# Attention and expert layer on one core: every transposition moves from the DMA queue to TensorE

## The chip, the cores and the metric

The kernel runs on one core of one Trainium2 chip. The time is the device time of one execution in microseconds (us); less is better. Before the change it is 672.57 us, the median of 3 runs that lie between 672.4 and 672.64 us. The engines are named as the profile names them: PE (TensorE, matrix products), PEld (its path for loading the stationary operand), DVE (VectorE), ACT (ScalarE), POOL (GpSimd), SP (SyncE, which here only issues DMAs).

## What is computed

One post-norm layer over x of shape (2, 512, 512): two batches of 512 positions with 512 features. Attention has 32 query heads and 8 key/value heads of 128 features each, with a causal mask. Behind it stands a dense layer with eight low-rank experts whose weights come from a sparsemax.

```python
q = (x @ Wq)  # 32 heads of 128
k = (x @ Wk)  # 8 heads, each serves 4 query heads
v = (x @ Wv)
scores = where(causal, einsum('bhqd,bhkd->bhqk', q, k) * scale, -inf)
out = softmax(scores) @ v
x = layernorm(x + out @ Wo)
base = x @ W_base.T + b_base
weights = sparsemax(x @ W_router.T + b_router)
expert = einsum('bser,bse,ero->bso', einsum('bsd,edr->bser', x, lora_A), weights, lora_B)
x = layernorm(x + base + expert)
```

## The kernel before

**Two halves of everything.** Every operand of a product is kept as two float16 numbers, a high and a low part, and a product a·b is made of three matmuls: high·high, high·low and low·high (`mm3`, L228). That is why matmul counts are multiples of three. Only key/value group 0 is projected in another way, directly from float32 data (`park`, the `xr`/`wr` tiles), while the scales of the split are still being found.

**Groups and units.** There are 16 groups (g, b): 8 key/value heads g by 2 batches b. A group has four units i = 0 to 3. Unit i is a block of 128 rows of each of the four query heads, that is, positions 128·i to 128·i+127, and it attends to the keys up to its own end. So unit 0 is the smallest and unit 3 the largest.

**The work of a group.** `proj` (L321) makes K (`j` = 4), V (`j` = 5) and four Q heads (`j` = 0 to 3) out of the transposed x: 12 matmuls of 512 columns each into a PSUM tile of the tag "pj", which has two buffers. `cut_psum` (L233) empties that tile: ACT writes the high half, then DVE the low half. V comes out of `mul_v` with features on the partitions, so it must be transposed: `turn_v` (L303) makes three more variants of it with four ACT copies (L312 to L315: `twice`, `once`, `four`, packings for the diagonal blocks) and one DMA transposition of all 20 blocks (L318).

**The work of a unit.** `unit_a` (L333): scores S (12 matmuls of 32 to 512 columns, into tag "S", four buffers), a minimum by DVE (L396), the exponential by ACT (L401), and then `cut_p`, which writes P's high and low halves into the tile `phl` (ACT L360, L368; DVE L363), as 8·i+6 float16 blocks of 128 by 128. Two DMA transpositions a unit (L389) turn those blocks into `pt`. `unit_b` (L416): P·V, 6 to 24 matmuls of 128 or 256 columns, with `vt` as the stationary and `pt` as the moving operand, into the tag "PV" (one buffer), emptied by `cut_psum` into `o`. `unit_c` (L457): 12 matmuls of 512 columns with the output weights into the tag "wo" (one buffer), and DVE adds the result to the residual row `acc` (L470).

**The order.** The main loop (L932) runs over steps s. A step does `unit_a` of unit s; then, for the next group, some of its six projections (`(4, 0)`, `(1,)`, `(5,)`, `(2, 3)` in the steps with i = 0, 1, 2, 3); then `unit_b` of unit s−1; then `unit_c` of unit s−2. In between, `advance` prepares weights for later groups on POOL (`split16`: three instructions a tile, L119, L121, L122). Within this loop a planner sets the final order of each engine's queue; each engine executes its queue in order. `sync_load` puts loads on SP's queue behind the third last transposition (`hist`).

**The end.** The last group and the second halves of the tiles of rows run in an order written out by hand (`TAIL`, L895): a letter is a piece of work, the digit a tile of 128 rows (`a`, `p`, `q`: `unit_a`; `b`, `o`: `unit_b`; `c`, `d`: `unit_c`; `X`, `l`, `r`, `s`, `h`, `m`, `e`, `f`, `F`: the expert layer). The expert layer needs the normalized x transposed: `turn(t, True)` lets TensorE transpose four float32 blocks of a tile (L596, ACT L598, DVE L607), for tiles 3 to 7. For tiles 0 to 2 (`ffn`, L672) x is split first (ACT L602, POOL L609) and transposed by DMA (L610).

PSUM has eight buffers of 2 KB a partition, all taken: two "pj", four "S", one "PV", one "wo".

Of the kernel before, what the change touches and what calls it, by code (L numbers as in the profile page):

```python
# [17 lines left out]
P = 128  # L18
# [22 lines left out]
def kernel(  # L41
# [50 lines left out]
    def f(ap):  # L92
        return ap.bitcast(F32)

    hist = []
# [158 lines left out]
    def cut(b, g, j):  # L254
        return CUT if g else CK[b][:, j : j + 1]
# [38 lines left out]

    def mul_v(g, b, tag="pj"):
        pv = pj(f"pvp{g}_{b}", tag)
        project(pv, g, b, 5)
        return pv

    def end_v(g, b, pv):  # L300
        cut_psum(v2[:, 0, :], v2[:, 1, :], pv, cut(b, g, 5))

    def turn_v(g, b):  # L303


        r = 2 * R
        high, low, twice, once, four = (v2[:, k, :].rearrange("p (t k) -> p t k", k=P) for k in range(5))

        def double(t, k):
            return high[:, :, :k].unsqueeze(2).broadcast_to([P, NT, t, k])  # L310

        nc.scalar.copy(twice.rearrange("p t (a k) -> p t a k", a=2), double(2, r))  # L312
        nc.scalar.copy(once[:, :, :r], low[:, :, :r])
        nc.scalar.copy(four.rearrange("p t (a k) -> p t a k", a=4)[:, :, ::3], double(2, R))
        nc.scalar.copy(four[:, :, R:r], low[:, :, :R])  # L315
        vt = sb.tile([P, 5 * NT, P], F16, tag="VT", name=f"vt{g}_{b}", bufs=2)
        with tc.issue_after(hist[-1]) if g == 0 and hist else nullcontext():
            sync_transpose(vt, v2.rearrange("p a s -> p (a s)"))  # L318
        VT[(g, b)] = vt

    def proj(g, b, j):  # L321
        if j == 4:
# [5 lines left out]
        else:  # L328
            end_q(g, b, j, mul_q(g, b, j))

    PT = {}

    def unit_a(g, b, i, whole=True):  # L333

# [7 lines left out]
        pt = sb.tile([P, nb, P], F16, tag="PT", name=f"pt{g}_{b}_{i}", bufs=2)  # L342
        es = []
        st = sb.tile([P, 4, 4], F32, tag="ast", name=f"ast{g}_{b}_{i}", bufs=3)
        full = i * P
# [1 line left out]
        def cut_p(h):  # L347
# [5 lines left out]
            for j in (h, h + 1):  # L353
# [30 lines left out]
                if i:  # L384
                    low(lows[:, :full], 0, full)
                low(p[:, full + (3 - j) * R : full + P][:, : n - full], full, n - full)

            on = slice(0, 2 * m) if h == 0 else slice(2 * m, nb)
            sync_transpose(pt[:, on], phl[:, on.start * P : on.stop * P])  # L389

        for j in range(4):
            n = full + (j + 1) * R
            qh, ql = (q2[:, a, HPG * i + j].rearrange("p h q -> p (h q)") for a in range(2))
# [10 lines left out]
            es.append(sc)  # L404
            if whole and j % 2:
                cut_p(j - 1)
        PT[(g, b, i)] = pt
        yield
        if not whole:
            for h in (0, 2):  # L410
                cut_p(h)
                yield

    OT = {}

    def unit_b(g, b, i):  # L416
        vt = VT[(g, b)]
        pt = PT.pop((g, b, i))
        pv = ps.tile([P, HPG, 4, R], F32, tag="PV", name=f"pv{g}_{b}_{i}")
        dst = pv.rearrange("p h j q -> p j h q")  # L420
        m = 2 * i + 1

        def blocks(start, step):
            return pt[:, start : start + step + 1 : step].rearrange("p j (h q) -> p j h q", q=R)

        def three(kt, start, step):
            vh, vl = vt[:, kt, :], vt[:, NT + kt, :]
# [9 lines left out]
        twice, once, four = (vt[:, k * NT + i, :] for k in (2, 3, 4))  # L437
# [152 lines left out]
    def turn(t, urgent=False):  # L590
        a = acc[t]
        X[t] = x2 = sb.tile([P, 2 * KC, P], F16, tag="raw", name=f"x2{t}", bufs=6)
        if urgent:
            px = ps.tile([P, KC, P], F32, tag="S", name=f"px{t}", bufs=4)
            for c in range(KC):
                nc.tensor.transpose(px[:, c, :], a[:, c * P : (c + 1) * P], ident)  # L596
            H[t] = px
            nc.scalar.copy(x2[:, :KC, :], px)  # L598
        else:
            xn = sb.tile([P, 2, HID], F16, tag="raw", name=f"xn{t}", bufs=6)  # L600
            H[t] = xn
            nc.scalar.copy(xn[:, 0], a)  # L602

    def low(t, engine):
        x2, src = X[t], H[t]
        if src.dtype == F32:
            nc.vector.tensor_tensor(x2[:, KC:, :], src, x2[:, :KC, :], ALU.subtract)  # L607
        else:
            engine.tensor_tensor(src[:, 1], acc[t], src[:, 0], ALU.subtract)  # L609
            sync_transpose(x2, src.rearrange("p a d -> p (a d)"))  # L610

    PA, PB, H = {}, {}, {}

# [58 lines left out]
    def ffn(t):  # L672
# [2 lines left out]
        yield  # L675
        with behind(mybir.EngineType.DVE):
            normalize(a, a, st)
        turn(t)
        low(t, nc.gpsimd)
        for _ in range(5):  # L680
            yield
        with behind(mybir.EngineType.PE):
            lora_in(t, False)
# [209 lines left out]


    TAIL = """  # L895
    n3 a7 C6 N3 B7 p7 q7 O7 X3 l3 D6 a6 r3 C7 s3 b7 p6 q6 D7 h3 o7 m3 a5 p5 c7 b6 q5 e3 d7 o6 n7
    a4 c6 N7 p4 q4 b5 f3 X7 l7 m7 o5 r7 d6 n6 s7 c5 N6 d5 h7 X6 n5 l6 b4 e7 o4 f7 r6 c4 N5 F7 s6
    F3 X5 l5 d4 n4 m6 h6 r5 m5 s5 N4 e6 f6 h5 X4 l4 F6 e5 r4 s4 f5 m4 h4 F5 e4 f4 F4
    """

    def tail():
# [2 lines left out]
        A = {first + i: unit_a(g, b, i, False) for i in range(NT)}  # L904
        B = {first + i: unit_b(g, b, i) for i in range(NT)}
        C = {first + i: unit_c(g, b, i, i == NT - 1) for i in range(NT)}
        B6 = {first + NT - 1: unit_b(*groups[-2], NT - 1)}
        C6 = {first + i: unit_c(*groups[-2], i, False) for i in (NT - 2, NT - 1)}
        pieces = dict.fromkeys("apq", A) | dict.fromkeys("bo", B) | dict.fromkeys("cd", C)
        pieces |= dict.fromkeys("BO", B6) | dict.fromkeys("CD", C6)  # L910
        work = {
            "l": lambda t: low(t, nc.vector), "L": lambda t: low(t, nc.gpsimd),
            "s": route, "e": lora_part, "x": turn, "X": lambda t: turn(t, True),
            "r": lambda t: lora_in(t, t >= NT), "m": lambda t: base_part(t, True), "h": lambda t: lora_mid(t, t >= NT),
        }
        stats = {}
# [15 lines left out]
    for s in range(len(units) - NT):  # L932
        if s < len(units):
            g, b, i = units[s]
            k = s // NT
            nx = groups[k + 1] if k + 1 < len(groups) else None
            done(unit_a(g, b, i))
            step_live()
            if nx:
                for j in ((4, 0), (1,), (5,), (2, 3))[i]:  # L940
                    proj(*nx, j)
                    advance()
            step_live()
        if s >= LB:
            done(unit_b(*units[s - LB]))
            step_live()
            advance()
# [66 lines left out]
```

## Time and profile before

| | |
|---|---|
| median of 3 runs | 672.57 us (672.4 to 672.64) |
| the profiled execution, its own time | 674.08 us |
| its span, first to last instruction | 672.3 us |
| mean granted TensorE clock | 0.996 |
| transposing DMAs | 128 of P, 16 of V, 3 of x, all on SP's queue |
| median from issue to landing | P 3.6 us, V 5.3 us, x 2.9 us |
| POOL, instructions before the change | 405 |

The profile is of one execution, whose time is 1.5 us above the median; 1.8 us of it lie outside the span. A group of instructions is given as line, engine, operation, what it writes and reads, count, busy time and the mean duration of one. A matmul's duration reaches from its start until its last result has drained; matmuls that follow each other overlap, so the distance between two starts is what one of them costs the engine, and it is found from a run of n matmuls as (length of the run − duration of one) / (n − 1).

### The profile page before, as it was taken

What the parts mean: (1) busy time and instruction counts of PE and PEld (TensorE: products, weight loads), DVE (VectorE), ACT (ScalarE), POOL (GpSimd) and SP (SyncE); (2) the same over time, 40 slices, a digit from 0 to 9 for tenths busy, and PEclk for the clock granted to TensorE, in tenths of its full rate; (3) what the DMA queues carried; (4) which work ended last, traced back from release to release, by engine and by line L of the source; (5) the groups of instructions that cost most, each with busy time, mean ns of one, the idle gap of its engine ahead of it and who ended that gap; (6) DMA issues with size and microseconds to landing.
All of it is one profiled execution on the core that took longest, in us unless ns stands there. A gap on an engine that the chain in (4) does not pass through costs nothing. (4 is left out here: it accounts for less than half of the span.)

```text
span 672.3 us, 12440 instructions
## 1 busy us (share of the span) xinstructions
PE 652.2 (97%) x3946; PEld 374.7 (56%) x3946; DVE 520.8 (77%) x1698; ACT 388.5 (58%) x1196; POOL 259.2 (39%) x405
## 2 busy tenths in 40 slices
PE   8899999999999999999999999999899999999995
PEld 5666555555555555555555655555465555555552
DVE  5788687968696686978788787868767687878796
ACT  6886574847374774747466475726656484545510
POOL 5658550634227199543318058053505011100011
PEclk9899999999999999999999999999999999999999
DMA  8659483656739374655739363653828164563311
GB/s 310 173 158 208 100 182 78 148 84 128 147 63 231 89 148 101 115 130 98 177 40 254 74 145 72 129 146 58 176 39 142 24 126 75 88 129 75 71 40 52
DMA packets 213538, 81.06 MB, mean 121 GB/s; under 512 B 198112, under 2 KB 198368, under 8 KB 213472
## 3 DMA queue, kind: packets, MB, share of 16 engines
q1 hardware_dynamic: 213472, 80.26, 56.2%
q8 instruction: 31, 0.51, 0.3%
q14 instruction: 35, 0.29, 0.2%
HBM read 29.12 MB, written 2.10 MB: 46 GB/s over the span
## 5 line engine op out<-in xcount | busy, mean ns | idle before, releaser
L401 ACT ACTIVATE s<-s,ast 128x320 f32<-128x320 f32 (+15 forms) x256 | 117.6, 460 | 149.8 <-DVE ast L396 145.1
L231 PE MATMUL pw<-w,o 128*128 128x512 f16 x768 | 177.0, 379 | 0.3 <-DVE acc L470 0.3
L231 PEld LDWEIGHTS <-w 128*128 128x128 f16 x1008 | 98.0, 98 | 110.7
L231 PE MATMUL pq<-xT,w 128*128 128x512 f16 x672 | 152.4, 379 | 0.0
L363 DVE SCALAR_TENSOR_TENSOR phl<-s,ast,phl 128x128 f16<-128x128 f32 (+7 forms) x352 | 125.1, 417 | 33.9 <-ACT phl L360 31.3
L360 ACT ACTIVATE phl<-s,ast 128x96 f16<-128x96 f32 (+11 forms) x304 | 117.3, 478 | 9.1 <-DVE ast L350 6.0
L231 PEld LDWEIGHTS <-o 128*128 128x128 f16 x768 | 74.8, 98 | 77.8 <-issue 0.8
L396 DVE CUSTOM_DVE_ANT_0 s<-s,mask,lm 128x320 f32<-128x320 f32 (+15 forms) x256 | 113.3, 502 | 1.9 <-PE s L231 1.3
L231 PE MATMUL s<-k,q 128*128 128x480 f16 (+15 forms) x768 | 103.1, 279 | 5.7 <-DVE phl L363 1.9
L231 PE MATMUL pv<-pt,vt 128*128 128x256 f16 (+1 forms) x960 | 105.6, 262 | 2.9 <-DMA pt<-phl 1.5
L231 PEld LDWEIGHTS <-vt 128*128 128x128 f16 x960 | 86.1, 99 | 22.5 <-issue 4.3
L231 PEld LDWEIGHTS <-q 128*128 128x128 f16 x768 | 62.7, 98 | 45.3 <-issue 4.1
L263 POOL TENSOR_SCALAR lm<-sc,xs 128x1 f32<-128x1 f32 x15 | 4.0, 268 | 206.7 <-DVE sc L139 103.0
L122 POOL TENSOR_TENSOR w<-raw,w 128x512 f16<-128x512 f32 x70 | 79.8, 1164 | 0.2
L119 POOL TENSOR_SCALAR raw<-raw,sc 128x512 f32<-128x512 f32 x70 | 48.0, 698 | 53.6 <-issue 39.0
L470 DVE SCALAR_TENSOR_TENSOR acc<-pw,lm,acc 128x512 f32<-128x512 f32 x64 | 47.7, 745 | 19.6 <-PE pw L231 19.3
L236 DVE SCALAR_TENSOR_TENSOR o<-pv,o 128x512 f16<-128x512 f32 x64 | 43.6, 682 | 24.1 <-ACT o L235 24.0
L235 ACT ACTIVATE o<-pv 128x512 f16<-128x512 f32 x64 | 40.0, 625 | 24.3 <-PE pv L231 24.1
L401 ACT ACTIVATION_READ_ACCUMULATOR s<-s,ast 128x1 f32 x256 | 51.3, 200 | 0.0
L125 DVE TENSOR_REDUCE mx<-raw 128x1 f32<-128x512 f32 x68 | 44.1, 675 | 8.0 <-DMA raw<-in_wo_dram 7.8
L236 DVE SCALAR_TENSOR_TENSOR q<-pq,q 128x512 f16<-128x512 f32 x56 | 37.4, 682 | 9.5 <-ACT q L235 9.5
L348 DVE RECIPROCAL ast<-ast 128x2 f32<-128x2 f32 x128 | 20.9, 163 | 29.8 <-ACT s L401 28.5
(172 smaller groups left out, 675.3 us busy)
## 6 DMA issues: line engine op xcount, KB each, us to landing
raw<-in_wo_dram SPq DMA_DIRECT2D x32, 256.0 KB, 3.4
raw<-in_wq_dram SPq DMA_DIRECT2D x29, 256.0 KB, 4.6
xraw<-in_xt_dram SPq DMA_DIRECT2D x8, 256.0 KB, 5.2
raw<-in_wk_dram SPq DMA_DIRECT2D x8, 256.0 KB, 3.8
raw_x<-in_xt_dram SPq DMA_DIRECT2D x8, 256.0 KB, 4.7
acc<-in_x_dram SPq DMA_DIRECT2D x8, 256.0 KB, 5.1
pt<-phl SPq DMA_TRANSPOSE x128, 3.6
out_dram<-y SPq DMA_DIRECT2D x8, 256.0 KB, 2.0
```

Of the source, the lines that this page charges most:

```text
L119: nc.gpsimd.tensor_scalar(view, view, by, 1.0, ALU.mult, ALU.mult)
L122: return first.ins, nc.gpsimd.tensor_tensor(lo, view, hi, ALU.subtract).ins
L125: nc.vector.tensor_reduce(dst, view, AX.X, ALU.max, apply_absolute_value=True)
L231: nc.tensor.matmul(dst, a, b, start=first and j == 0, stop=last and j == n - 1)
L235: nc.scalar.activation(hi, psrc, AF.Copy, scale=by)
L236: return nc.vector.scalar_tensor_tensor(lo, psrc, by, hi, ALU.mult, ALU.subtract).ins
L348: nc.vector.reciprocal(st[:, 2, h : h + 2], st[:, 1, h : h + 2])
L360: nc.scalar.activation(dst, src, AF.Copy, scale=by)
L363: nc.vector.scalar_tensor_tensor(dst, src[:, at : at + k], by, p[:, at : at + k], ALU.mult, ALU.subtract)
L396: nc.vector.tensor_tensor_reduce(out=sc[:, :n], in0=sc[:, :n], in1=mask[:, S - n :], scale=lm[:, 0:1], scalar=BIG, op0=ALU.add, op1=ALU.mi ...
L401: nc.scalar.activation(sc[:, :n], sc[:, :n], AF.Exp, bias=st[:, 0, j : j + 1], scale=-1.0, accum_out=st[:, 1, j : j + 1])
L470: nc.vector.scalar_tensor_tensor(a, pw, LM[(g, b)][:, 7:8], a, ALU.mult, ALU.add)
```

## The change

No DMA transposes any more; `hist` and `sync_transpose` go, and loads are no longer held behind transpositions.

*P.* A new generator `unit_t` has TensorE transpose the blocks of `phl`, eight at a time, against a float16 identity (`ident16`, made once by POOL) into a PSUM tile `px`, and ACT copies that tile to `pt` (`turn_blocks`). In the main loop its first pieces stand before the projections of the step, one piece before each projection; what is left comes right before `unit_b`, which now stands behind `unit_c`. `px` takes the tag "pj" in the main loop.

*V.* For g > 0 `mul_v` exchanges the operands: x is stationary, the weights move, so keys come out on the partitions and no transposition is needed; it takes 48 matmuls of 128 columns in place of 12 of 512. For g = 0 TensorE transposes the eight blocks. The variants `twice`, `once`, `four` are made by six POOL copies in place of four ACT copies, in two standing tiles `vts`, of which each group uses the other.

*x.* `turn` always goes through TensorE, and `low` always through DVE, also for tiles 0 to 2.

*The end.* `T` and `t` in `TAIL` are the pieces of `unit_t`.

```diff
-    v2 = const.tile([P, 5, S], F16, tag="v2", name="v2")
-    nc.gpsimd.memset(v2[:, 3:, :], 0.0)
+    ident16 = const.tile([P, P], F16, tag="ident16", name="ident16")
+    nc.gpsimd.tensor_scalar(ident16, ident, 1.0, 1.0, ALU.mult, ALU.mult)
+    vts = [const.tile([P, 5, NT, P], F16, tag=f"vt{k}", name=f"vt{k}") for k in range(2)]
+    for vt in vts:
+        nc.gpsimd.memset(vt[:, 3:], 0.0)
...
     def sync_load(dst, src):
-        with tc.issue_after(hist[-3]) if len(hist) > 2 else nullcontext():
-            return nc.sync.dma_start(dst, src)
-
-    def sync_transpose(dst, src):
-        hist.append(nc.sync.dma_start_transpose(dst, src).ins)
+        return nc.sync.dma_start(dst, src)
...
-            with behind(mybir.EngineType.DVE) if g > 1 and not rows else nullcontext():
+            with behind(mybir.EngineType.DVE) if g > 1 or rows else nullcontext():
                 amax(mx[:, j : j + 1], raw)
...
     def mul_v(g, b, tag="pj"):
         pv = pj(f"pvp{g}_{b}", tag)
-        project(pv, g, b, 5)
+        if not g:
+            project(pv, g, b, 5)
+            return pv
+        w2, x2 = W[(g, 5)], xT[b]
+        for t in range(NT):
+            on = slice(t * P, t * P + P)
+            pairs = []
+            for c in range(KC):
+                pairs += [(x2[:, q, c, on], w2[:, r, c, :]) for q, r in ((0, 0), (0, 1), (1, 0))]
+            mm3(pv[:, on], pairs)
         return pv
...
     def turn_v(g, b):
+        vt = vts[groups.index((g, b)) % 2]
+        if not g:
+            src = VT[(g, b)].rearrange("p a s -> p (a s)")
+            turn_blocks(vt[:, :2].rearrange("p a t d -> p (a t) d"), src)
+        VT[(g, b)] = vt
+        high, low, twice, once, four = (vt[:, k] for k in range(5))
+        def copy(dst, src):
+            nc.gpsimd.tensor_scalar(dst, src, 1.0, 1.0, ALU.mult, ALU.mult)
         r = 2 * R
...
+        for k in range(2):
+            copy(twice[k * r : k * r + r], high[:r])
+        copy(once[:r], low[:r])
+        copy(four[:R], high[:R])
+        copy(four[R:r], low[:R])
+        copy(four[P - R :], high[:R])
+
+    def turn_blocks(dst, src, tag="pj"):
+        n = dst.shape[1]
+        px = ps.tile([P, 8, P], F16, tag=tag, name="px", bufs=4 if tag == "S" else 2)
+        for k in range(n):
+            nc.tensor.transpose(px[:, k, :], src[:, k * P : (k + 1) * P], ident16)
+        nc.scalar.copy(dst, px[:, :n, :])
...
-            on = slice(0, 2 * m) if h == 0 else slice(2 * m, nb)
-            sync_transpose(pt[:, on], phl[:, on.start * P : on.stop * P])
...
+    def unit_t(g, b, i, tag="pj"):
+        phl = PH.pop((g, b, i))
+        nb = 8 * i + 6
+        PT[(g, b, i)] = pt = sb.tile([P, nb, P], F16, tag="PT", name=f"pt{g}_{b}_{i}", bufs=2)
+        for k in range(0, nb, 8):
+            n = min(nb, k + 8)
+            turn_blocks(pt[:, k:n, :], phl[:, k * P : n * P], tag)
+            yield
...
     TAIL = """
+    n3 a7 T7 C6 T7 N3 T7 D6 T7 B7 p7 q7 O7 X3 l3 a6 t7 C7 t7 r3 s3 t7 D7 t7 p6 q6 b7 h3 t6 o7 t6
+    m3 t6 a5 c7 b6 p5 q5 e3 d7 t5 o6 n7 t5 a4 c6 N7 p4 q4 b5 f3 X7 t4 l7 m7 o5 r7 d6 n6 s7 c5 N6
...
             done(unit_a(g, b, i))
             step_live()
+            turns = unit_t(*units[s - LB]) if s >= LB else iter(())
             if nx:
                 for j in ((4, 0), (1,), (5,), (2, 3))[i]:
+                    next(turns, None)
                     proj(*nx, j)
                     advance()
             step_live()
-        if s >= LB:
-            done(unit_b(*units[s - LB]))
...
         if s >= LC:
...
+        if s >= LB:
+            done(turns)
+            done(unit_b(*units[s - LB]))
+            step_live()
+            advance()
```

More of the change, by code (lines that the diff above doesn't have):

```diff
@@ L93, in f @@
         return ap.bitcast(F32)
-    hist = []
     def sync_load(dst, src):
-        with tc.issue_after(hist[-3]) if len(hist) > 2 else nullcontext():
-            return nc.sync.dma_start(dst, src)
-    def sync_transpose(dst, src):
-        hist.append(nc.sync.dma_start_transpose(dst, src).ins)
+        return nc.sync.dma_start(dst, src)
     def load_raw(src, name, rows=False):
@@ L296, in mul_v @@
         pv = pj(f"pvp{g}_{b}", tag)
-        project(pv, g, b, 5)
+        if not g:
[8 more added lines that the diff above has]
+            mm3(pv[:, on], pairs)
         return pv
     def end_v(g, b, pv):
-        cut_psum(v2[:, 0, :], v2[:, 1, :], pv, cut(b, g, 5))
@@ L303, in turn_v @@
-    def turn_v(g, b):
-        r = 2 * R
[L307 to L319, printed above, removed]
+        vt = vts[groups.index((g, b)) % 2].rearrange("p a t d -> p a (t d)")
@@ new lines, in end_v @@
+        dst = vt
+        if not g:
+            dst = sb.tile([P, 2, S], F16, tag="v2", name=f"v2{b}", bufs=1)
+        cut_psum(dst[:, 0, :], dst[:, 1, :], pv, cut(b, g, 5))
+        VT[(g, b)] = dst
+    def turn_v(g, b):
+        vt = vts[groups.index((g, b)) % 2]
+        if not g:
+            src = VT[(g, b)].rearrange("p a s -> p (a s)")
[4 more added lines that the diff above has]
+            nc.gpsimd.tensor_scalar(dst, src, 1.0, 1.0, ALU.mult, ALU.mult)
+        r = 2 * R
+        for k in range(2):
[4 more added lines that the diff above has]
+        copy(four[P - R :], high[:R])
@@ L329, in proj @@
             end_q(g, b, j, mul_q(g, b, j))
-    PT = {}
+    PT, PH = {}, {}
     def unit_a(g, b, i, whole=True):
@@ L341, in unit_a @@
         phl = sb.tile([P, nb * P], F16, tag="PHL", name=f"phl{g}_{b}_{i}", bufs=2)
-        pt = sb.tile([P, nb, P], F16, tag="PT", name=f"pt{g}_{b}_{i}", bufs=2)
         es = []
@@ L406, in unit_a @@
                 cut_p(j - 1)
-        PT[(g, b, i)] = pt
+        PH[(g, b, i)] = phl
         yield
@@ L426, in three @@
         def three(kt, start, step):
-            vh, vl = vt[:, kt, :], vt[:, NT + kt, :]
+            vh, vl = vt[:, 0, kt, :], vt[:, 1, kt, :]
             ph, pl = (blocks(at, step) for at in (start + kt, start + kt + i + 1))
@@ L435, in unit_b @@
             mm3(dst[:, :2], pairs, last=False)
-        twice, once, four = (vt[:, k * NT + i, :] for k in (2, 3, 4))
+        twice, once, four = (vt[:, k, i, :] for k in (2, 3, 4))
         p0, p1 = (pt[:, k, :].rearrange("p (h q) -> p h q", q=R) for k in (i, m + i))
@@ L592, in turn, with low @@
         X[t] = x2 = sb.tile([P, 2 * KC, P], F16, tag="raw", name=f"x2{t}", bufs=6)
[L593 to L610, printed above, removed]
+        px = ps.tile([P, KC, P], F32, tag="S" if urgent else "pj", name=f"px{t}", bufs=4 if urgent else 2)
+        for c in range(KC):
+            nc.tensor.transpose(px[:, c, :], a[:, c * P : (c + 1) * P], ident)
+        H[t] = px
+        nc.scalar.copy(x2[:, :KC, :], px)
+    def low(t):
+        x2 = X[t]
+        nc.vector.tensor_tensor(x2[:, KC:, :], H[t], x2[:, :KC, :], ALU.subtract)
     PA, PB, H = {}, {}, {}
@@ L677, in ffn @@
             normalize(a, a, st)
-        turn(t)
-        low(t, nc.gpsimd)
-        for _ in range(5):
+        for _ in range(2):
+            yield
+        with behind(mybir.EngineType.PE):
+            turn(t)
+        low(t)
+        for _ in range(3):
             yield
@@ L895 @@
     TAIL = """
-    n3 a7 C6 N3 B7 p7 q7 O7 X3 l3 D6 a6 r3 C7 s3 b7 p6 q6 D7 h3 o7 m3 a5 p5 c7 b6 q5 e3 d7 o6 n7
-    a4 c6 N7 p4 q4 b5 f3 X7 l7 m7 o5 r7 d6 n6 s7 c5 N6 d5 h7 X6 n5 l6 b4 e7 o4 f7 r6 c4 N5 F7 s6
-    F3 X5 l5 d4 n4 m6 h6 r5 m5 s5 N4 e6 f6 h5 X4 l4 F6 e5 r4 s4 f5 m4 h4 F5 e4 f4 F4
+    n3 a7 T7 C6 T7 N3 T7 D6 T7 B7 p7 q7 O7 X3 l3 a6 t7 C7 t7 r3 s3 t7 D7 t7 p6 q6 b7 h3 t6 o7 t6
+    m3 t6 a5 c7 b6 p5 q5 e3 d7 t5 o6 n7 t5 a4 c6 N7 p4 q4 b5 f3 X7 t4 l7 m7 o5 r7 d6 n6 s7 c5 N6
+    d5 h7 X6 n5 l6 b4 e7 o4 f7 r6 c4 N5 F7 s6 F3 X5 l5 d4 n4 m6 h6 r5 m5 s5 N4 e6 f6 h5 X4 l4 F6
+    e5 r4 s4 f5 m4 h4 F5 e4 f4 F4
     """
@@ L906, in tail @@
         C = {first + i: unit_c(g, b, i, i == NT - 1) for i in range(NT)}
+        T = {first + i: unit_t(g, b, i, "pj" if i == NT - 1 else "S") for i in range(NT)}
+        T6 = {first + NT - 1: unit_t(*groups[-2], NT - 1)}
         B6 = {first + NT - 1: unit_b(*groups[-2], NT - 1)}
         C6 = {first + i: unit_c(*groups[-2], i, False) for i in (NT - 2, NT - 1)}
-        pieces = dict.fromkeys("apq", A) | dict.fromkeys("bo", B) | dict.fromkeys("cd", C)
+        pieces = dict.fromkeys("apq", A) | {"t": T, "T": T6} | dict.fromkeys("bo", B) | dict.fromkeys("cd", C)
         pieces |= dict.fromkeys("BO", B6) | dict.fromkeys("CD", C6)
         work = {
-            "l": lambda t: low(t, nc.vector), "L": lambda t: low(t, nc.gpsimd),
-            "s": route, "e": lora_part, "x": turn, "X": lambda t: turn(t, True),
+            "l": low, "s": route, "e": lora_part, "X": lambda t: turn(t, True),
             "r": lambda t: lora_in(t, t >= NT), "m": lambda t: base_part(t, True), "h": lambda t: lora_mid(t, t >= NT),
@@ L943 @@
             step_live()
-        if s >= LB:
-            done(unit_b(*units[s - LB]))
-            step_live()
-            advance()
         if s >= LC:
```

## The prediction

> **What bounds the kernel now.** I read the busy time of each engine first, then the same by stage, then the waits of PE, then runs of equal matmuls.
>
> ```profile
> PE 652.2 (97%) x3946; PEld 374.7 (56%) x3946; DVE 520.8 (77%) x1698; ACT 388.5 (58%) x1196; POOL 259.2 (39%) x405
> ```
>
> PE is busy 97% of the span. By stage (start, length, then PE, PEld, DVE, ACT, POOL busy with counts, granted clock, DMA share, GB/s):
>
> ```profile
> 0.00:40.00 40.00, 35.64 (x153) 25.43 (x154) 28.49 (x83) 31.31 (x80) 25.41 (x49) 0.96 0.79 258
> 40.00:220.00 180.00, 179.26 (x1099) 102.76 (x1098) 139.89 (x450) 109.43 (x344) 80.61 (x118) 1.00 0.65 133
> 240.00:400.00 160.00, 159.55 (x976) 89.84 (x974) 126.89 (x401) 95.64 (x302) 81.72 (x123) 1.00 0.64 133
> 420.00:600.00 180.00, 178.14 (x1097) 100.20 (x1096) 139.78 (x464) 103.77 (x321) 45.39 (x71) 1.00 0.53 101
> 600.00:672.00 72.00, 62.33 (x399) 35.12 (x396) 56.59 (x201) 22.96 (x71) 6.46 (x11) 0.99 0.30 66
> ```
>
> In the three long stretches PE idles 0.74, 0.45 and 1.86 us; only the start (4.4) and the end (9.7) leave holes. Busy need not mean useful, so I check the distance between starts.
>
> ```profile
> 317.38 5.34 PE L231 MATMUL pq<-xT,w 128*128 128x512 f16 x24
> 641.80 0.87 PE L231 MATMUL pb<-lar,x 128*128 128x136 f16 x12
> 303.77 0.66 PE L231 MATMUL pv<-pt,vt 128*128 128x128 f16 x6
> 326.96 0.62 PE L231 MATMUL s<-k,q 128*128 128x32 f16 x12
> 613.33 0.60 PE L596 MATMUL px<-ident,acc 128*128 128x128 f32 x4
> ```
>
> 512 columns: (5.34 − 0.379)/23 = 216 ns. 136 columns: (0.87 − 0.223)/11 = 59 ns, each with a new stationary operand. The pv run holds three matmuls of 128 and three of 256 columns; 0.66 − 0.27 = 0.39 us over five distances agrees with 56 and 109 ns. The scores of a unit 0 (mean 80 columns) stand (0.62 − 0.22)/11 = 36 ns apart, so loading a stationary operand (98 ns by itself) is hidden even there. PE works at about 0.42 ns a column, without bubbles. **Columns added to PE are therefore added to the span**, unless they fall into the 14 us of holes at the two ends.
>
> What the removed DMAs cost PE stands in its waits:
>
> ```profile
> PE pv L231 <- DMA pt<-phl: 1.5, 3, 0.9
> ACT phl L368 <- DMA pt<-phl: 16.2, 9, 4.4
> ```
>
> PE waited 1.5 us for transposed P, three times in all; ACT's 16.2 us lie on an engine with 42% idle. At most 1.5 us is to be won.
>
> **The change part by part.** *P, removed:* 128 transposing DMAs on SP; gain 0 to 1.5 us, I take 0. *P, added:* a group has 6 + 14 + 22 + 30 = 72 blocks, 16 groups 1152. No float16 transposition is in the trace. The two nearest rows are the float16 matmul of 128 columns (56 ns) and the float32 transposition of 128 columns, (0.60 − 0.273)/3 = 109 ns. I take 56: the float32 one lasts 273 ns, as long as a float16 matmul of 256 columns (272), which looks like two passes over four-byte data; a float16 128-column matmul lasts 219. 1152 × 56 ns = **64.5 us**; upper end 1152 × 109 ns = 125.6 us. Nothing hides it.
>
> The Trainium skill ("TensorE: Matmul & The Clock Gate", Part 4: PE-mode transpose) speaks against the change: it gives about 275 ns for a transposition inside a kernel and says that such work doesn't wake the clock gate. By that the estimate would be 1152 × 275 ns = 317 us more, about 990 us; the float32 transpositions here stand 109 ns apart at clock 0.99, which contradicts reading 275 ns as a distance.
>
> *V, g > 0:* 14 groups × (48 × 56 ns − 12 × 216 ns) = 14 × 0.096 = **1.3 us**. *V, g = 0:* 2 × 8 × 56 ns = **0.9 us**. *x of tiles 0 to 2:* 12 float32 transpositions × 109 ns = **1.3 us**. Sum on PE: 64.5 + 1.3 + 0.9 + 1.3 = **68.0 us**.
>
> *ACT:* four V copies go: 0.67 + 0.47 + 0.47 + 0.36 = 1.96 us a group, −31.3 us. Copies of `px` come: six of 1024 and four of 768 elements a group. The copy of 512 from PSUM takes 0.59 us (L598); the slope of the exponential's row, (662 − 259)/480 = 0.84 ns an element, makes 1.02 and 0.80 us, so 16 × (6 × 1.02 + 4 × 0.80) = 149 us, and 2 for V of g = 0. ACT: 388.5 − 31 + 151 = 508 us, 68% of 750. *DVE:* three subtractions of 0.68 us more, 523 us. Neither becomes the bound as a sum. *POOL:* 96 copies, bounded by the smallest (0.28, L267) and the 512-element one (0.63, L121): 27 to 60 us more, minus 3.5 of x; I take 60, 316 us in all. V is needed by P·V only after two more steps, some 20 us later: 0. If POOL ran over, the first P·V of a group would wait. *SP:* loads no longer queue behind transpositions; PE waited for no load: 0. *`unit_c` ahead of `unit_b`:* its twelve matmuls read an `o` that is a step old, and its sum by DVE has a whole step until "wo" is needed again: 0. *The ordering of `amax` for the output weights:* DVE alone, 0.
>
> **The new wait.** `px` shares two "pj" buffers with the projections, and ACT's copy is queued behind the unit's softmax. In the step at 315.04 (unit 3, two projections) that looks so:
>
> ```profile
> 316.67 0.58 ACT L401 ACTIVATE s<-s,ast 128x416 f32<-128x416 f32 x1 [1.70 <-DVE ast L396]
> 319.26 2.46 ACT L360 ACTIVATE phl<-s,ast 128x384 f16<-128x384 f32 x5
> 321.57 0.63 ACT L235 ACTIVATE q<-pq 128x512 f16<-128x512 f32 x1
> ```
>
> Scores end at 317.38; first piece 8 × 56 ns, until 317.83; projection 12 × 216 ns, until 320.42. The second piece wants the first one's buffer, but ACT is in softmax until 321.72 and copies until 322.74: PE, behind whose head the second projection, `unit_c` and P·V are queued, would wait 2.3 us. If the planner puts `unit_c` (2.59 us, ready) in between, PE runs until 323.01 and the second piece until 323.46; the next projection waits for the other buffer: ACT's cut ends at 322.74 + 0.63, DVE's 0.68 later at 324.05, so 0.6 us. The next unit's scores may fill that. Such steps (i = 0 and 3) are two of four, 32 in all. Both ends: 0 and 32 × 2.3 = 74 us. The planner left almost no idle time on PE before, so I take the middle of 0 and 0.6 us: 32 × 0.3 = **9.6 us**. The last pieces of a step stand right before P·V, which reads their blocks last; what they could add lies inside the upper end.
>
> *The end:* 102 transpositions (5.7 of the 64.5 us) fall into the stretch with 9.7 us of holes; a DMA of 3.6 us turns into 0.45 + 1.02 us there. From −5.7 to the same upward, if hand-placed pieces meet a busy "pj"; I take 0.
>
> Sum: 68.0 + 9.6 = 77.6 us. On the profiled span that is 672.3 + 77.6 = 749.9; the execution is 1.8 us longer than its span and 1.5 over the median, so on the median of 672.57 it makes **750 us**.
>
> **Rivals.** *Late buffers (chance 0.19).* If ACT and DVE lag in all 64 steps by the 0.6 us of the walk, 38 us are added to 740.6: **779 us**; with 2.3 us in 32 steps 815. For it: ACT goes from 58% to 68% and every buffer is taken. Against: the planner's clean record. *Transpositions at half rate (0.12):* 109 ns, 61.1 us more than in my sum: **811 us**. For it: the only transpositions in the trace. Against: the two-pass reading. *Faster (0.04):* the transpositions slip into PE's idle time and all waits at the ends go with the DMAs' latency. PE idles 672.3 − 652.2 = 20.1 us; at 15 ns each, 672.6 − 20.1 + 1152 × 0.015 = **670 us**. It decides below 20.1/1152 = 17 ns a block. Against: matmuls of a mean of 80 columns cost 36 ns here. *Nothing moves (0.01):* some transpositions stay on DMA and their copies are never issued, 672.6; nothing in the diff leaves one.
>
> **How the numbers follow.** My forecast, 0.64, spans 736 (the end swallows its share, no late buffers) to 765. The range goes on into late buffers up to 798 and leaves out half rate (0.12), the worst of late buffers (0.03), faster and no change (0.05). A difference under 0.2% can't be told from none here. Slower by more: 0.64 + 0.19 + 0.12 = 0.95; within: 0.01; faster: 0.04.
>
> **What would show it.** Right: 1168 float16 transpositions in runs of eight with 56 ns between starts, PE busy near 720 us, ACT near 508, V's matmuls 672 of 128 columns. Idle time of PE before `px` or projections ended by ACT or DVE, in sum over 25 us, means late buffers. A run of eight lasting 0.98 instead of 0.61 us means half rate. I am wrong altogether if PE's busy time rises by much less than 60 us.

## The result, and the profile after

The changed kernel takes 780.6 us, the median of 4 runs (778.39 to 781.14); the kernel before took 672.49 us beside it. The ratio is 1.160, with a 95% interval from 1.158 to 1.163: 108 us more. The profiled execution after took 780.98 us, with a span of 779.2 us.

The page's first part and PE's own stages, of the changed kernel (start, length, then busy time and count of PE, PEld, DVE, ACT and POOL, granted clock, DMA share, GB/s):

```profile
PE 739.1 (95%) x5630; PEld 465.6 (60%) x5630; DVE 528.4 (68%) x1701; ACT 512.2 (66%) x1294; POOL 314.3 (40%) x500
```

```profile
0.00:40.00 40.00, 35.89 (x157) 25.86 (x158) 29.06 (x83) 29.85 (x74) 26.35 (x53) 0.91 0.74 262
40.00:250.00 210.00, 201.27 (x1556) 126.97 (x1555) 139.43 (x444) 150.02 (x386) 102.61 (x152) 0.99 0.15 44
250.00:450.00 200.00, 194.13 (x1556) 122.72 (x1555) 134.57 (x424) 132.33 (x338) 91.70 (x152) 1.00 0.11 31
450.00:650.00 200.00, 193.27 (x1518) 120.10 (x1517) 135.21 (x433) 138.67 (x352) 82.12 (x124) 1.00 0.07 20
650.00:700.00 50.00, 49.16 (x375) 30.39 (x374) 35.59 (x124) 25.96 (x63) 5.29 (x9) 1.00 0.03 12
700.00:779.00 79.00, 65.38 (x479) 39.59 (x476) 54.53 (x196) 35.41 (x85) 6.28 (x11) 0.96 0.06 21
```

PE did 1684 matmuls more (5630 − 3946) and lost its gapless middle: from 40 to 700 us it idles 8.7 + 5.9 + 6.7 + 0.8 = 22 us, where the same part of the kernel before had some 6. At the end it idles 13.6 us instead of 9.7. PE's busy time rose by 86.9 us, more than the columns account for, because a matmul ahead of a gap counts its whole drain as busy: one of 512 columns lasts 380 ns, while the next could start after 216. The gaps are therefore better found by subtraction: the span grew by 106.9 us, the columns by 68, so 39 us are new.

Not all of these 39 us are waiting. While PE works, the granted clock drops to 0.50 in one stretch of the kernel before and in three of the changed one (start, length and columns as above; the first row is the kernel before):

```profile
28.36:31.77 3.41, 3.41 (x10) 2.64 (x9) 2.43 (x19) 2.49 (x12) 3.10 (x8) 0.50 0.85 122
25.78:32.61 6.83, 6.33 (x29) 5.19 (x30) 5.66 (x24) 3.90 (x12) 5.91 (x9) 0.50 0.99 351
244.24:247.65 3.41, 3.41 (x29) 2.70 (x28) 1.70 (x11) 1.94 (x8) 1.50 (x6) 0.50 0.47 153
715.27:718.69 3.42, 3.42 (x16) 1.82 (x16) 1.91 (x8) 2.93 (x9) 0.00 (x0) 0.50 0.00 0
```

By the distances between starts the float16 matmuls of the changed kernel lose 4.2 us in these stretches, those of the kernel before nothing. Why the clock dropped was not looked into.

That the columns cost what the prediction said, two runs of matmuls in the time line of PE and the row of the copies show (time line: start, length of the run, what; row of the tile: count, then the shortest, median and longest duration in ns):

```profile
401.06 0.61 PE L340 MATMUL px<-ident,phl 128*128 128x128 f16 x8
401.51 2.84 PE L229 MATMUL pvp<-w,xT 128*128 128x128 f16 x48
```

```profile
L341 ACT COPY pt<-px x160: 789/1002/1271, 41.2 to 746.5; 128x1024 f16<-128x1024 f16 x96, 128x768 f16<-128x768 f16 x64
```

Eight transpositions: (0.61 − 0.22)/7 = 56 ns each. V's 48 matmuls: (2.84 − 0.22)/47 = 56 ns. The copies last 1.00 and 0.79 us, 1.02 and 0.80 were worked out.

**Where the waiting sits.** What PE waited for, in the changed kernel (sum in us, times, longest):

```profile
PE pv L229 <- ACT pt L341: 5.7, 8, 2.2
PE tot L128 <- ACT sq L186: 4.4, 7, 0.8
PE pq L229 <- DVE k L234: 4.3, 11, 0.5
```

Three consumers wait: P·V for transposed P, the small matmul that sums the squared maxima for the scales, and a projection for its "pj" buffer. None is large in this view. It counts only the time in which nothing drains; by the distances between starts, the gaps are up to three times as long (the table at the end of the experiments). Next, what the other engines waited for. First the kernel before:

```profile
ACT s L401 <- DVE ast L396: 145.1, 59, 7.2
ACT o L235 <- PE pv L231: 24.1, 20, 1.9
ACT q L235 <- PE pq L231: 12.1, 15, 3.6
DVE s L396 <- PE s L231: 1.3, 2, 1.0
```

and the kernel after:

```profile
ACT q L233 <- PE pq L229: 61.0, 29, 2.8
ACT o L233 <- PE pv L229: 56.2, 47, 1.7
DVE s L413 <- PE s L229: 55.4, 38, 3.0
ACT pt L341 <- PE px L340: 43.6, 38, 3.6
ACT s L418 <- DVE ast L413: 30.0, 39, 1.6
```

Before, ACT waited above all for DVE, inside the softmax, and 36 us (24.1 + 12.1) for P·V and projections. After, ACT waits 161 us for PE's results (61.0 + 56.2 + 43.6) and DVE 55 us for scores. By themselves these sums show no loop: with P back on DMA (the second run of that kind below, 1.4% over the kernel before) ACT waits as long for PE:

```profile
ACT o L239 <- PE pv L235: 128.5, 48, 7.0
```

The chain that ended last, followed back from the last instruction (engines' shares of the span), tells the two apart: first the changed kernel, then the one with P on DMA, of which the view follows a smaller part of the span:

```profile
PE 35%; ACT 32%; DVE 18%; issue 5%; POOL 2%; DMA 0%; POOLq 0%; ACTq 0%; DVEq 0%
PE 49%; DVE 9%; ACT 3%; issue 3%; POOL 1%; DMA 1%; POOLq 0%; DVEq 0%; ACTq 0%
```

With TensorE transposing, ACT's work stands in the chain for a third of the span, beside PE's: PE waits for ACT and ACT waits for PE. One step shows this loop (time line of all engines, cut; brackets: idle time before, and what ended it):

```profile
407.07 0.49 PE L340 MATMUL px<-ident,phl 128*128 128x128 f16 x6
407.18 1.02 ACT L381 ACTIVATE phl<-s,ast 128x352 f16<-128x352 f32 x2 [0.88 <-DVE tot L133]
...
407.90 0.52 PE L229 MATMUL s<-k,q 128*128 128x416 f16 x2
...
408.09 0.80 ACT L341 COPY pt<-px 128x768 f16<-128x768 f16 x1
...
408.94 0.82 PE L229 MATMUL pv<-pt,vt 128*128 128x256 f16 x6 [0.53 <-ACT pt L341]
...
409.60 0.72 PE L229 MATMUL s<-k,q 128*128 128x416 f16 x3
```

The last piece of P is transposed at 407.57. ACT is in the softmax of the running unit until 408.20, copies, and P·V goes on at 408.94. The planner filled the gap with two matmuls of the next unit's scores, too few; the rest of these scores stands behind P·V in PE's queue. So, as I read it, the next softmax starts late, and with it the next copies. Over the whole stretch from 50 to 700 us a copy starts 0.50 us, on average, after the last transposition of its `px` has ended.

### The profile page after: what moved, and what is told of

Read it like the earlier page. It is cut to its first block, busy times and chain, and to the rows that moved or that the text cites. A ratio compares the mean times of both kernels' runs of the same rounds, so it can differ in the third digit from the quotient of the medians.

```text
span 779.2 us, 15455 instructions
## 1 busy us (share of the span) xinstructions
PE 739.1 (95%) x5630; PEld 465.6 (60%) x5630; DVE 528.4 (68%) x1701; ACT 512.2 (66%) x1294; POOL 314.3 (40%) x500
## 4 chain that ended last, share of the span: by engine, by line
PE 35%; ACT 32%; DVE 18%; issue 5%; POOL 2%; DMA 0%; POOLq 0%; ACTq 0%; DVEq 0%
PE pq L229 11%; ACT s L418 10%; ACT pt L341 9%; ACT phl L381 8%; PE pw L229 7%; PE pv L229 7%; PE s L229 3%; DVE s L413 3%; PE px L340 3%; DVE mx L123 2%; ACT q L233 2%; DVE phl L384 2%; DVE q L234 2%; PE pa L229 2%; DVE o L234 1%
## 5 line engine op out<-in xcount | busy, mean ns | idle before, releaser
L229 PE MATMUL pw<-w,o 128*128 128x512 f16 x768 | 182.3, 380 | 0.0
L341 ACT COPY pt<-px 128x1024 f16<-128x1024 f16 (+1 forms) x160 | 148.1, 937 | 44.0 <-PE px L340 43.6
L413 DVE CUSTOM_DVE_ANT_0 s<-s,mask,lm 128x320 f32<-128x320 f32 (+15 forms) x256 | 118.9, 502 | 56.0 <-PE s L229 55.4
L229 PEld LDWEIGHTS <-w 128*128 128x128 f16 x840 | 80.4, 98 | 100.8 <-issue 15.1
L229 PE MATMUL pv<-pt,vt 128*128 128x256 f16 (+1 forms) x960 | 113.8, 262 | 8.8 <-ACT pt L341 5.7
L325 POOL TENSOR_SCALAR vt<-vt 64x512 f16<-64x512 f16 (+1 forms) x96 | 58.2, 611 | 144.5 <-ACT vt L233 121.0
L229 PE MATMUL s<-k,q 128*128 128x32 f16 (+15 forms) x768 | 109.3, 281 | 5.1 <-ACT pt L341 1.5
L340 PEld LDWEIGHTS <-phl 128*128 128x128 f16 x1152 | 76.7, 99 | 28.9 <-issue 4.5
L340 PE MATMUL px<-ident,phl 128*128 128x128 f16 x1152 | 90.3, 220 | 3.2 <-ACT pt L341 2.0
L229 PEld LDWEIGHTS <-q 128*128 128x128 f16 x768 | 63.2, 99 | 28.1 <-issue 5.2
L233 ACT ACTIVATE o<-pv 128x512 f16<-128x512 f32 x64 | 38.6, 602 | 59.4 <-PE pv L229 56.2
L233 ACT ACTIVATE q<-pq 128x512 f16<-128x512 f32 x56 | 34.5, 616 | 60.1 <-PE pq L229 60.1
```

The lines of the kernel that those rows point to most:

```text
L229: nc.tensor.matmul(dst, a, b, start=first and j == 0, stop=last and j == n - 1)
L233: nc.scalar.activation(hi, psrc, AF.Copy, scale=by)
L325: nc.gpsimd.tensor_scalar(dst, src, 1.0, 1.0, ALU.mult, ALU.mult)
L340: nc.tensor.transpose(px[:, k, :], src[:, k * P : (k + 1) * P], ident16)
L341: nc.scalar.copy(dst, px[:, :n, :])
L413: nc.vector.tensor_tensor_reduce(out=sc[:, :n], in0=sc[:, :n], in1=mask[:, S - n :], scale=lm[:, 0:1], scalar=BIG, op0=ALU.add, op1=ALU.mi ...
```

## The experiments

Each run is the changed kernel with one edit, unless said otherwise. Ratios are to the kernel before, measured beside it on the same chip (its medians were 672.87, 673.52, 672.65 and 672.29 us in the four batches).

**One of eight blocks transposed** (of P alone; V of g = 0 stays whole).

```diff
-    def turn_blocks(dst, src, tag="pj"):
+    def turn_blocks(dst, src, tag="pj", all_of_them=True):
...
-        for k in range(n):
+        few = n if all_of_them else 1
+        for k in range(few):
             nc.tensor.transpose(px[:, k, :], src[:, k * P : (k + 1) * P], ident16)
-        nc.scalar.copy(dst, px[:, :n, :])
+        nc.scalar.copy(dst, px[:, :n, :] if few == n else px[:, :1, :].broadcast_to([P, n, P]))
...
-            turn_blocks(pt[:, k:n, :], phl[:, k * P : n * P], tag)
+            turn_blocks(pt[:, k:n, :], phl[:, k * P : n * P], tag, False)
```

> Of each px only the first block is transposed (160 instead of 1152 transpositions of P); ACT copies as many elements as before, all from that block, so P is wrong beyond it. Theory A (columns at 56 ns plus waits for late buffers): 992 x 56 ns = 55.6 us go from PE; since PE then reaches the copies earlier, the waits stay or grow a little: 725 to 740 us. Rival B (a transposition costs more than its distance of 56 ns, as all of the 108 us spread over 1152 blocks, 94 ns each): 993/1152 of it goes, 687 us. Rival C (ACT is now the bound, with 512 us busy and its own waits): the time hardly falls, over 765 us.

738.63 us, ratio 1.098 (1.094 to 1.102): 42.0 us less for 55.6 us of columns taken away. Theory A holds, at the upper end; a price of 94 ns a block does not. 13.6 us came back, most of it as waiting, and the largest wait of PE is now a projection for a buffer that waits for ACT's copy:

```profile
PE pq L229 <- ACT pt L342: 9.5, 8, 1.6
```

**Every block transposed twice.**

```diff
-    def turn_blocks(dst, src, tag="pj"):
+    def turn_blocks(dst, src, tag="pj", times=1):
...
         for k in range(n):
-            nc.tensor.transpose(px[:, k, :], src[:, k * P : (k + 1) * P], ident16)
+            for _ in range(times):
+                nc.tensor.transpose(px[:, k, :], src[:, k * P : (k + 1) * P], ident16)
...
-            turn_blocks(pt[:, k:n, :], phl[:, k * P : n * P], tag)
+            turn_blocks(pt[:, k:n, :], phl[:, k * P : n * P], tag, 2)
```

> Every block of P is transposed twice in a row into the same place; the copies stay as they are. 1152 transpositions more at 56 ns make 64.3 us of PE work. PE alone the bound: 845 us, or up to 10 us less where the second one falls into a wait. ACT in part the bound (as 42 us for 55.6 us of columns taken away says): 825 to 835 us.

837.91 us, ratio 1.247 (1.244 to 1.250): 57.3 us more for 64.3 us of columns, within the first expectation, not the second. Sixteen transpositions in a row last 1.06 us, again 56 ns each:

```profile
407.06 1.06 PE L341 MATMUL px<-ident,phl 128*128 128x128 f16 x16
```

So nine tenths of added columns go to the time and three quarters of removed ones come off it: PE is the bound, but not alone.

**ACT copies one block of each px** (of P alone).

```diff
+    pts = [const.tile([P, 30, P], F16, tag=f"pts{k}", name=f"pts{k}") for k in range(2)]
+    for pt in pts:
+        nc.gpsimd.memset(pt, 0.0)
...
-        nc.scalar.copy(dst, px[:, :n, :])
+        few = n if all_of_them else 1
+        nc.scalar.copy(dst[:, :few], px[:, :few, :])
...
-        PT[(g, b, i)] = pt = sb.tile([P, nb, P], F16, tag="PT", name=f"pt{g}_{b}_{i}", bufs=2)
+        PT[(g, b, i)] = pt = pts[units.index((g, b, i)) % 2][:, :nb]
...
-            turn_blocks(pt[:, k:n, :], phl[:, k * P : n * P], tag)
+            turn_blocks(pt[:, k:n, :], phl[:, k * P : n * P], tag, False)
```

> All blocks are transposed, but ACT copies only the first block of each px into two standing pt tiles that are set to zero once, so P.V reads zeros elsewhere. A copy falls from 0.94 us to about 0.36. Theory A: the 40 us of PE waits that are new come from copies that stand late in ACT's queue and hold a pj buffer or P.V; most of them go, 745 to 755 us. Rival D (the 40 us are the planner's order, POOL's copies of V or anything else that does not hang on the copies): 775 to 781 us.

765.87 us, ratio 1.138 (1.135 to 1.140): 14.7 us less, between the two theories. The edit has a cost of its own: POOL zeroes the two tiles for 6.5 us near the start, ahead of work for the first group, and PE has a single wait there that the changed kernel does not show:

```profile
4.89 6.54 POOL L93 MEMSET pts<- 128x3840 f16 x2
```

```profile
PE tot L131 <- ACT xT L119: 4.8, 1, 4.8
```

Whether that wait comes from the zeroing was not tried; by the trace DVE stands 2.6 us behind a load there, in an order of its queue that the changed kernel does not have. Without it, short copies are worth some 20 us. The length of the copies explains a third to half of the 39 us, not all.

**Half of each copy by DVE** (and the maxima's condition as before, see below).

```diff
-        nc.scalar.copy(dst, px[:, :n, :])
+        half = n // 2
+        nc.scalar.copy(dst[:, :half], px[:, :half, :])
+        nc.vector.tensor_copy(dst[:, half:], px[:, half:n, :])
```

> The maxima's condition as before, and each px is emptied half by ACT and half by DVE at the same time. Theory A (a copy that is late and long holds up PE): a copy takes some 0.6 instead of 0.94 us and ACT is rid of 60 to 75 us, 758 to 766 us. Rival (DVE, busy 68%, is as late as ACT, and now both have to come): 773 to 785 us.

782.11 us, ratio 1.163 (1.160 to 1.166): nothing gained, in the rival's range. The copies did become short, on both engines:

```profile
L342 ACT COPY pt<-px x160: 468/581/650, 39.1 to 750.5; 128x512 f16<-128x512 f16 x96, 128x384 f16<-128x384 f16 x64
L343 DVE COPY pt<-px x160: 332/412/426, 39.6 to 751.0; 128x512 f16<-128x512 f16 x96, 128x384 f16<-128x384 f16 x64
```

But DVE is in the same softmax loop; what ACT was spared, DVE had to do between two steps of that loop. By the table below, the gaps ahead of P·V and of projections shrank to less than half, and those ahead of scores and transpositions grew by more.

**px in the tag of the scores.**

```diff
-    def unit_t(g, b, i, tag="pj"):
+    def unit_t(g, b, i, tag="S"):
...
-        T6 = {first + NT - 1: unit_t(*groups[-2], NT - 1)}
+        T6 = {first + NT - 1: unit_t(*groups[-2], NT - 1, "pj")}
```

> In the main loop px takes the tag S (four buffers, with the scores) instead of pj (two, with the projections). Theory A1 (the projections wait for a pj buffer that px or its successor holds, 12 to 13 us in the trace): these waits go and few new ones come, 764 to 770 us. Theory A2 (the lateness of ACT's copy itself counts, above all ahead of P.V, not whose buffer it holds): 775 to 785 us. Rival: scores now wait for S, over 790 us.

777.1 us, ratio 1.155 (1.152 to 1.157): 3.5 us less, as theory A2 has it. The wait for a "pj" buffer turned into a wait for one of "S", which DVE frees at the end of the softmax:

```profile
PE px L340 <- DVE phl L384: 12.4, 27, 4.8
```

**The copies ahead of other work of ACT in the planner.**

```diff
-        nc.scalar.copy(dst, px[:, :n, :])
+        with tc.high_priority():
+            nc.scalar.copy(dst, px[:, :n, :])
```

> The copies of px get a higher priority in the planner, so they stand in ACT's queue as soon as their transpositions end, ahead of the softmax of the unit that runs. Theory A (the copy stands behind the softmax, that is the whole cost): 750 to 765 us. Rival F (the softmax comes later by as much, and the next scores and P with it): 776 to 790 us.

778.8 us, ratio 1.159 (1.156 to 1.161): the 1.8 us less are no gain that can be told. The time fits rival F, but the test is a weak one. Over the stretch from 50 to 700 us the copies do start earlier, 0.36 us after the last transposition's end instead of 0.50; at the place shown above, though, the order stayed as it was (ACT's time line):

```profile
404.29 1.02 ACT L382 ACTIVATE phl<-s,ast 128x352 f16<-128x352 f32 x2 [0.88 <-DVE tot L133]
405.21 0.80 ACT L342 COPY pt<-px 128x768 f16<-128x768 f16 x1
```

**unit_b ahead of unit_c, as before.**

```diff
+        if s >= LB:
+            done(turns)
+            done(unit_b(*units[s - LB]))
+            step_live()
+            advance()
         if s >= LC:
...
-        if s >= LB:
-            done(turns)
-            done(unit_b(*units[s - LB]))
-            step_live()
-            advance()
```

> The changed kernel with unit_b ahead of unit_c, as in the kernel before. The last pieces of a step then come right behind the last projection and P.V right behind them, with no unit_c ahead to cover ACT's copies. If unit_c's place is what keeps the waits at 40 us: 795 to 815 us. If the planner pulls unit_c forward by itself wherever PE would wait: 777 to 786 us.

784.62 us, ratio 1.165 (1.160 to 1.169): 4 us more, at the edge of what these runs can tell (781.25 to 786.45 against 778.39 to 781.14), and in the range for a planner that moves unit_c by itself. The moved step is worth little.

**All pieces ahead of unit_c.**

```diff
+        if s >= LB:
+            done(turns)
         if s >= LC:
...
         if s >= LB:
-            done(turns)
             done(unit_b(*units[s - LB]))
```

> All pieces of unit_t that are left after the projections stand ahead of unit_c instead of behind it, so that its 2.59 us on PE can cover ACT's copies before P.V reads them. Theory A (P.V waits because its last copy comes too late; 11.0 us of PE gaps from scores to P.V and 4.9 within P.V in the trace): most of these 16 us go, 764 to 770 us. Rival F (ACT's softmax and PE wait for each other in a loop, so that a gap closed here opens elsewhere): 776 to 783 us.

773.78 us, ratio 1.151 (1.149 to 1.154): 6.8 us less, between the two. Some 2 of the 6.8 us may be the granted clock: the profiled executions lose 4.2 and 1.8 us in stretches at 0.50. P·V's waits for the copy fell from 5.7 to 2.5 us by the trace, and those of the projections for a buffer that a copy holds rose from 1.6 to 3.3:

```profile
PE pq L229 <- ACT pt L341: 3.3, 4, 1.5
...
PE pv L229 <- ACT pt L341: 2.5, 2, 2.3
```

**P by DMA again, the rest of the change kept.**

```diff
+    hist = []
+
     def sync_load(dst, src):
-        return nc.sync.dma_start(dst, src)
+        with tc.issue_after(hist[-3]) if len(hist) > 2 else nullcontext():
+            return nc.sync.dma_start(dst, src)
+
+    def sync_transpose(dst, src):
+        hist.append(nc.sync.dma_start_transpose(dst, src).ins)
...
+            on = slice(0, 2 * m) if h == 0 else slice(2 * m, nb)
+            sync_transpose(pt[:, on], phl[:, on.start * P : on.stop * P])
...
-        for k in range(0, nb, 8):
-            n = min(nb, k + 8)
-            turn_blocks(pt[:, k:n, :], phl[:, k * P : n * P], tag)
-            yield
+        return
+        yield
```

> P is transposed by DMA again, right after its halves are written as in the kernel before, and loads queue behind the transpositions as there; V by keys, POOL's six copies, x of tiles 0 to 2 through TensorE and unit_c ahead of unit_b stay. Theory A: P alone carries 64.5 us of columns and the waits for its copies, so 675 to 682 us are left. Rival D: V by keys with POOL's copies, or the order of unit_c and unit_b, carries a good part of the 40 us: 690 to 715 us.

687.48 us, ratio 1.023 (1.020 to 1.026). P's way through TensorE costs 780.6 − 687.5 = 93.1 us; the loads, which are held behind transpositions again, are in that difference and were not tried apart. But 687.5 lies above what theory A allows and below what D asks for: 14.6 us over the kernel before stay, where 3.5 us of columns were counted. One wait of PE stands out:

```profile
PE tot L134 <- ACT sq L192: 7.0, 7, 2.8
```

**The same, with the maxima's condition as before.**

```diff
-            with behind(mybir.EngineType.DVE) if g > 1 or rows else nullcontext():
+            with behind(mybir.EngineType.DVE) if g > 1 and not rows else nullcontext():
```

> P by DMA again, and the maxima's condition as before; V by keys, POOL's copies, x through TensorE and the order of unit_c and unit_b stay. Theory E: 687.5 falls to 678 to 681 us, of which 2.8 are columns. Rival D2 (the order of unit_c and unit_b or POOL's copies cost what is left over 675): 684 to 688 us.

682.44 us, ratio 1.014 (1.011 to 1.017), between the two expectations: 5.0 us less, and that wait is gone from the list. The prediction had put this edit at nothing. About 5 us above the columns remain; 3.4 of them are gaps by the table below, not ahead of any one consumer, and the rest is open.

**That condition alone, in the changed kernel.**

> The changed kernel with one condition as before: the maxima over the output weights are no longer queued behind DVE's last instruction. Theory E (that edit, which the prediction put at nothing, makes TensorE's small matmul for the scales wait for DVE and ACT, some 7 us in the trace): 771 to 775 us. Rival: the wait only moves on to the next projection or P.V, 778 to 781 us.

780.88 us, ratio 1.160 (1.158 to 1.163): no difference, as the rival has it. The waits of that matmul are gone, but a new one came once, near the start, where DVE stands behind a maximum whose weights have not landed:

```profile
44.56 0.69 DVE L123 TENSOR_REDUCE mx<-raw 128x1 f32<-128x512 f32 x1 [6.73 <-DMA raw<-in_wo_dram]
```

So the condition guards the start, and with P on DMA it costs later; the next run keeps the guard and drops the rest, together with the pieces ahead of unit_c.

```diff
-            with behind(mybir.EngineType.DVE) if g > 1 or rows else nullcontext():
+            with behind(mybir.EngineType.DVE) if (g > 1) != rows else nullcontext():
```

> As the run with the pieces ahead of unit_c, and the maxima over the output weights are held behind DVE's last instruction for g = 0 and 1 alone, where without it DVE sat 6.7 us behind a load; for g > 1 they are free, as in the kernel before. Theory E (for g > 1 the condition makes the scales' matmul wait for ACT, about 7 us of PE gaps before and behind it in the trace): 765 to 769 us. Rival F (the gap opens elsewhere): 772 to 776 us.

774.24 us, ratio 1.152 (1.150 to 1.153): no better than the pieces ahead of unit_c alone. The scales' wait is gone from PE's list, that of the projections for a copy rose to 4.1 us and "px" has one of 2.4 us for DVE. Rival F holds here: closing the scales' gap leaves the time as it was. No version beats the kernel before.

**Where the gaps went.** The distances of the prediction (36, 56, 59 and 216 ns for 80, 128, 136 and 512 columns) fit 0.417 ns a column and 2.5 ns a matmul. What a distance between two starts has over that, if it is more than 15 ns, is a gap. The table sums the gaps behind float16 matmuls by what comes next, in us, for one profiled execution each; matmuls that start in stretches at a granted clock of 0.50 are left out, and what they lose stands in the last column.

| run | P·V | projections | transpositions of P | scores | scales | other | sum | clock 0.50 |
|---|---|---|---|---|---|---|---|---|
| kernel before | 3.8 | 0.0 | none | 6.1 | 1.1 | 3.9 | 14.9 | 0.0 |
| changed kernel | 15.7 | 13.2 | 5.6 | 4.9 | 6.6 | 2.6 | 48.6 | 4.2 |
| ACT copies one block | 4.9 | 8.1 | 5.8 | 3.0 | 4.5 | 1.8 | 28.1 | 2.6 |
| half of each copy by DVE | 6.0 | 3.3 | 15.9 | 17.5 | 2.4 | 3.8 | 49.0 | 7.5 |
| px in the tag of the scores | 10.8 | 0.2 | 25.4 | 4.7 | 2.2 | 2.1 | 45.3 | 3.6 |
| all pieces ahead of unit_c | 5.7 | 16.8 | 8.7 | 5.0 | 5.3 | 2.6 | 44.0 | 1.8 |
| the same, scales' maxima free | 5.8 | 16.4 | 11.2 | 5.0 | 1.7 | 2.5 | 42.6 | 2.6 |
| P by DMA, condition as before | 2.5 | 0.2 | none | 6.8 | 1.1 | 7.8 | 18.3 | 0.8 |

From the kernel before to the changed one the gaps grow by 34 us and the loss at half clock by 4, which together make the 39 us, within 1. The gaps stand in four places, and an edit that closes them in one opens them in another; only shorter copies on ACT bring the sum down far.

## Why the prediction was right, and where it was not

*The bound.* Right. PE had no bubbles to fill, and the columns had to be paid: 56 ns a transposition and 56 ns a matmul of V, as taken; half rate (109 ns) is out. The sum on PE of 68.0 us stands. The 275 ns of the Trainium skill ("TensorE: Matmul & The Clock Gate", Part 4: PE-mode transpose) is near the 219 ns that one transposition lasts here, but they start 56 ns apart at a granted clock of 0.99 to 1.00, so it is no price for one, and the measurement decides.

*What stood in for the DMAs.* Right: with P back on DMA most of the loss goes. The 1.5 us that PE had waited for DMAs were little to win.

*The other engines' sums.* ACT 508 us foretold, 512 measured; DVE 523 and 528; POOL 316 and 314. None is full. That did not make them harmless.

*The new wait.* The mechanism was named, its size was wrong: 9.6 us were taken, 39 us came, which puts the time into the stated range but past the 736 to 765 us of the forecast itself. The step that failed reads "The planner left almost no idle time on PE before, so I take the middle of 0 and 0.6 us: 32 × 0.3". By the table the 39 us have four parts, and the sum of the four is a little over 39. Ahead of projections and transpositions, the place that this term is about, 19 us came (13.2 + 5.6) for the 9.6. Ahead of P·V, 12 us came (15.7 − 3.8), where the prediction took nothing and left it to the upper end. Ahead of the scales' matmul 5.5 us came, from the order of the maxima, which was put at nothing. Some 4 us are the granted clock, which the prediction does not speak of; ahead of scores and the rest the gaps shrank by 2.5 us. Waits occur in the steps with one projection too (the one shown has i = 2 running into i = 3).

The rival "late buffers" comes out at 779 us, almost the measured time, but that is luck in part: it puts all 38 us on "pj" buffers, and its own sign, over 25 us of idle time of PE before `px` or projections ended by ACT or DVE, is not met. The wait rows of the changed kernel give some 12 us, the table 19. PE's busy time, foretold near 720 us, is 739.1, since drains ahead of gaps count as busy.

Of the 39 us, 34 come with P: 780.9 against 682.4 us with the maxima's condition as before in both, less 64.5 of columns. The argument from the planner's record was wrong, as I read it: before, PE's work depended on DMAs that ran beside the softmax; after, it depends on ACT, which is in the softmax.

*The edits put at nothing.* The order of the maxima costs 5.0 us where P goes by DMA, by the two runs; where P goes through TensorE, dropping it gains nothing, by two others. The place of unit_c, also put at nothing, gains up to 4 us, at the edge of the noise.

*The end.* Taken as 0; PE's holes there grew from 9.7 to 13.6 us.

*What stays open.* No single wait carries the 39 us. Short copies are worth 15 to 20 us, an earlier place for them some 5 to 7 with the clock's share in it, another buffer 3.5, and copies shared with DVE or put first in the planner nothing that can be told. At one place in the time line PE has ready work behind the matmul that waits: from 415.08 nine of unit_c's twelve matmuls run, then a projection waits for DVE until 417.37, and the other three come only behind it. That points to the fixed order of PE's queue, laid out for times that ACT and DVE do not quite keep; an order made by hand was not tried.

## What to carry to other kernels

Work moved onto an engine that is busy without bubbles costs its full column time, here 68 us; a DMA queue that does the same work beside it is worth keeping, even though each of these DMAs takes 3.6 us. When a transposition moves from DMA to TensorE, count the copy out of PSUM as a new dependence of TensorE on the engine that makes it, and ask where that engine is in its queue at that moment, not how busy it is on average. A planner's clean record holds for the dependences it had. And before a small gap is closed, look at the sum of the gaps by place: here they mostly moved.

## What the runs showed of the hardware

Float16 transpositions of 128 by 128 blocks follow each other at 56 ns, each with its own stationary operand, also sixteen in a row and between other matmuls, at a granted clock of 0.99 to 1.00; float32 ones stand at 109 ns, (0.60 − 0.273)/3 in the kernel before. DVE copies 512 float16 elements a partition out of PSUM in 0.41 us, ACT takes 0.58 us for the same (the run with shared copies); ACT needs 1.00 us for 1024 (the changed kernel) and 0.27 us for 128 (the run with one block).
